# Where two kinds of stores stand in a cross-attention and MLP kernel: block 14's weight sums, and a tile of tokens at the end of a batch

## The chip, the core and the metric

The kernel runs on one core of a Trainium2 chip. The core has TensorE (PE, matrix products into PSUM; its weight loads are a row of their own, PEld), VectorE (DVE), ScalarE (ACT), GpSimd (POOL), and SyncE (SP), which here only issues DMA transfers. Sixteen DMA engines move the data for all of them. Each engine works through its own instructions in order, and waits on semaphores for the others.

The metric is the device time of one execution in microseconds (us), the median of several runs. Everything is computed in float32.

## The reference

A cross-attention block followed by an MLP, with B = 4 batches, L = 512 tokens, D = 512 features, 16 heads of 32 features, and an inner size of 2048:

```python
x = layer_norm(hidden_states, ln1_w, ln1_b)
q = heads(x @ q_w + q_b)
k = heads(encoder_hidden_states @ k_w + k_b)
v = heads(encoder_hidden_states @ v_w + v_b)
attn = softmax(mask(q @ k.T * scale))
hidden = (attn @ v).merge() @ cproj_w + cproj_b + hidden_states
y = layer_norm(hidden, ln2_w, ln2_b)
y = gelu(y @ fc_w + fc_b) @ proj_w + proj_b
return hidden + y
```

## The kernel before

The attention runs in 32 blocks, numbered p = 0 to 31. A block is half of the queries of one head group: w = p // 2 counts batch and group (four groups of four heads in each batch), and p % 2 is the half. `block` (from L349) computes the scores and their softmax (`soften`), and transposes the probabilities on DVE into a tile tb. The blocks leave TensorE time for other matrix work, so each block has a list of fillers (`put(p, ...)`): the projections of the next head groups, `cproj`, and, from block 11 on, the MLP of batch 0 and half of that of batch 1. A filler is a function; what stands in a list is issued in that order, and this sets the order on every engine.

A block's probabilities are used two blocks later. `attend(w, half)` multiplies them with v (tile av, L429). Before, `copies` (from L397) moves tb into a tile pT: four copies within the same partitions on POOL (L405), and twelve DMA transfers across partitions on SP's queue (L410). There is one pT tile for most pairs, so the copies of pair p - 1 start when `attend` of pair p - 2 has read the tile, at the opening of block p. The loop over p at the end of `xattn_block` does this at each opening: `run(ahead[p])`, `attend` of the pair that is due, `fc_sums`, then the block itself.

The MLP's products are made by Winograd's form of Strassen's method: seven half-size products in place of eight, with sums of the operands made beforehand. Four steps matter here.

- `fc_sums` (L704) makes, for a pair of chunks of fc_w (raw in pbt), four sums of weights on POOL: three go to one of the two buffers of wsum, and one replaces a part of the raw chunk. For batch 0 the sums are also stored to DRAM (`sums_dram`, tile ws), with two DMA transfers issued from POOL: L714 with 384 KB, L715 with 128 KB. There are eight pairs, so sixteen such transfers. They are loaded again for batches 2 and 3 (L841), long after. `fc_sums` keeps up to two pairs ahead of the products.
- `fc_by_pair` uses the sums on TensorE (q, L671), and `load_mlp` then loads the next weights into the place of the used ones (L614, on SP's queue).
- `proj_sums` (called by `pre(...)`) makes the sums of the projection's operands on POOL: x and y into ptt, and differences in place into gt and pbt. In block 14 the filler `pre(0, 0)` is last in the list; `x1` just before it issues four loads of the next batch's tokens on SP's queue (L187).
- `proj` for batch 0 issues the seven products q1j to q7j (L777) in block 15 and adds them to the result. At quarter 3 two of the adds are put off by `S["late"]`, and block 29 calls them.

Block 10 calls `fc_sums` as a filler and makes the sums of the first two pairs there; the later pairs are made at the openings of the blocks.

After the attention, `last_mlps` runs the rest of batch 1's MLP and batches 2 and 3. Its second matrix product, `project`, is split once more: for batches 2 and 3 each of the seven products is itself made of seven, by `forty_nine` (from L889; L904 is its matmul). Its results go to three PSUM tiles of four quarters each and to r34: r1 and r26 come from one set of four banks (`acc_tile`), r57 and r34 from the other (`half_tile`, four tiles in turn). The last call in a batch is the one with `parts`: it adds each quarter straight to the result, where `parts` are the four 128 by 128 pieces of 256 tokens and 256 features (two pieces to a tile of 128 tokens). Behind it two transfers (L1028) store these pieces, one for each 128 tokens.

Of the kernel before, what the change touches and what calls it, by code (L numbers as in the profile page):

```python
# [20 lines left out]
P = 128  # L21
# [32 lines left out]
def xattn_block(ctx: ExitStack, tc: tile.TileContext, x, rawT, encT, mask, q_w, k_w, v_w, c_w, fc_w, p_w, vecs, rows, out):  # L54
    nc = tc.nc
# [44 lines left out]
    def mlp_w(n):  # L100
        return pbt[:, (n + MW) * D : (n + MW + 1) * D]
# [16 lines left out]
    S = {"gelu": [], "late": []}  # L118
# [472 lines left out]
    for name, b, i, *_ in products:  # L591
        n = 2 if name == "fc" else FQ
        done += 2 if name == "fc" else 1
        n = range(i * n, (i + 1) * n)
        if (name, b) == ("p", 0) and _[0] == 2:
            n = n[2:]
# [3 lines left out]
    n = next(i for i, w in enumerate(weights) if w[:2] == ("p", SPLIT))  # L600
    weights[n : n + FQ] = weights[n + 2 : n + FQ] + weights[n : n + 2]
    free = [
        next((o[3] for o in reversed(weights[:i]) if o[4] == w[4]), -1) for i, w in enumerate(weights)
    ]

    def load_mlp(most=len(weights)):

        end = min(count[0] + most, len(weights))
        while count[0] < end and free[count[0]] < count[1]:
            name, b, f, _, n = weights[count[0]]  # L610
            w = mlp_w(n)
            if name == "fc":
                w = w.rearrange("p (d f) -> p d f", d=ND)
            Q[0].dma_start(out=w, in_=fc_w[:, f, :, :] if name == "fc" else p_w[ts(f, P), :])  # L614
            S[name + "w", b, f] = w if name == "fc" else n + MW
            count[0] += 1

    NP = NF // 2
    HL = L // 2
# [4 lines left out]
    def add(engine, o, x0, x1):  # L624
        engine.tensor_tensor(o, x0, x1, ALU.add)  # L625

    def a_sums(a11, a12, a21, a22, s1, s2, s3, s4, engine=None):
        add(engine or nc.vector, s1, a21, a22)
        sub(s3, a11, a21, engine)
        sub(s2, s1, a11, engine)  # L630
        sub(s4, a12, s2, engine)
# [66 lines left out]
    sums_dram = dram.tile([NP, P, 4, 2, P], F32, tag="ws", name="ws")  # L698
    fc_pairs = [(0, c) for c in range(NP)] + [(SPLIT, c) for c in range(FIRST * FQ // 2)]

    def raw_pair(b, c):
        return [S["fcw", b, 2 * c + i] for i in range(2)]

    def fc_sums(ahead=2):  # L704

        while count[3] < len(fc_pairs) and count[3] < count[4] + ahead:
            b, c = fc_pairs[count[3]]
            if ("fcw", b, 2 * c + 1) not in S:
                return
            x, y = raw_pair(b, c)  # L710
            s = wsum[:, count[3] % 2]
            a_sums(x[:, :2], x[:, 2:], y[:, :2], y[:, 2:], s[:, 0], s[:, 1], y[:, :2], s[:, 2], nc.gpsimd)
            if b == 0:
                nc.gpsimd.dma_start(out=sums_dram[c, :, :3], in_=s)  # L714
                nc.gpsimd.dma_start(out=sums_dram[c, :, 3], in_=y[:, :2])  # L715
            S["ws", b, c] = s[:, 0], s[:, 1], y[:, :2], s[:, 2]
            count[3] += 1

    def fc_by_pair(b, c):
        q, k = divmod(2 * c, FQ)  # L720
        fc_seven(b, c, gT[q % 2][:, k : k + 2, :], raw_pair(b, c), S["ws", b, c], acc_half, q % 2)
        count[1] += 2
        count[4] += 1
        if (b, c) != (SPLIT, 2):
            load_mlp()
# [105 lines left out]
    def store_out(b):  # L831
        for t in range(NT):
            nc.sync.dma_start(out=out[b, ts(t, P), :], in_=S["hid", b, t])
# [15 lines left out]
    def last_mlps():  # L849
# [8 lines left out]
        p1p, u2p, u3p = (last.tile([P, 2, HL], F32, tag=n, name=n) for n in ("p1p", "u2p", "u3p"))  # L858
# [7 lines left out]
        def more(i):  # L866
            if i == 5:
                return S["more"]
            return [w_more[:, 4 * n : 4 * n + 4] if i == 4 else tt[:, i, n] for n in range(3)]

        def quarters(m):
            return [m[:, i * NP // 2 : (i + 1) * NP // 2, ts(j, P)] for i in range(2) for j in range(2)]
# [13 lines left out]
            sub(x21, x11, x21)  # L886
            sub(s4, x12, s2, nc.gpsimd)

        def forty_nine(b, name, o, x, w, free, i, parts=None):  # L889

            x11, s3, x12, x22 = quarters(x)
            s1, s2, s4 = free if isinstance(free, list) else quarters(free)[:3]
            w11, t3, w21, w22 = quarters(w)
            t1, t2, t4 = more(i)
            r1, r26 = (acc_tile(f"{n}{name}_{b}").rearrange("p (i n) -> p i n", i=4) for n in ("r1", "r26"))
            r57, r34 = (
                half_tile(f"{n}{name}_{b}").rearrange("p i (j n) -> p (i j) n", j=2) for n in ("r57", "r34")
            )
            o = o.rearrange("p t (j n) -> p (t j) n", j=2)
            p1 = p1s[:, i % 2]  # L900

            def product(r, x, w):
                for c in range(NP // 2):
                    nc.tensor.matmul(r, x[:, c], w[:, c], start=(c == 0), stop=(c == NP // 2 - 1))  # L904

            product(r1[:, 0], x11, w11)
            nc.scalar.copy(p1, r1[:, 0])
            product(r26[:, 0], x12, w21)
            product(r26[:, 1], s2, t2)
            add(nc.vector, o[:, 0:4:3], r26[:, :2], p1[:, None, :].broadcast_to([P, 2, P]))  # L910
            product(r57[:, 1], s3, t3)
            product(r57[:, 0], s1, t1)
            add(nc.vector, o[:, 1:3], r57[:, :2], o[:, 3:4].broadcast_to([P, 2, P]))
            add(nc.vector, o[:, 3], r57[:, 0], o[:, 2])
            if parts:
                for n, h in enumerate(parts):
                    add(nc.vector, h, o[:, n], h)
            product(r34[:, 0], s4, w22)
            product(r34[:, 1], x22, t4)
            if parts:  # L920
                for n in (1, 2):
                    add(nc.vector, parts[n], r34[:, n - 1], parts[n])
                return
            add(nc.vector, o[:, 1:3], r34[:, :2], o[:, 1:3])

        def half_tile(name):
# [11 lines left out]
        def project(b, pairs, sums, turns, middle):  # L938
            g11, g12, g21, g22 = (ga[:, :, k, j * HL : (j + 1) * HL] for j in range(2) for k in range(2))
            b11, b12, b21, b22 = (pb[:, :, k, j * HL : (j + 1) * HL] for k in range(2) for j in range(2))  # L940
            t1, t2, t3, t4 = pt[:, 0], pt[:, 1], b12, pt[:, 2]
            s1, s2, s3, s4 = gs[:, 0], gs[:, 1], g21, gs[:, 2]
# [8 lines left out]
            def hid(i, j, t):  # L951
                return S["hid", b, 2 * i + t][:, j * HL : (j + 1) * HL]
# [70 lines left out]
            if b > SPLIT:  # L1023
                parts = [hid(1, 0, t)[:, ts(j, P)] for t in range(2) for j in range(2)]
                middle()
                forty_nine(b, "4", u2p, g22, t4, s3, 5, parts)
                for t in range(2):
                    nc.sync.dma_start(out=out[b, ts(2 + t, P), :HL], in_=hid(1, 0, t))  # L1028
                return
            middle()  # L1030
            q4 = half_tile(f"q4p_{b}"), acc_half(f"q4p_{b}")
# [15 lines left out]
        for b, pairs, new in (  # L1047
            (SPLIT, range(half, NP), range(half)), (SPLIT + 1, range(NP), ()), (SPLIT + 2, range(NP), ())
        ):
            for c in pairs:  # L1050
# [6 lines left out]
                if new:  # L1057
                    n = (c - half + 2) % half
# [44 lines left out]
    def do(fn):  # L1103
        return [(0.0, fn)]
# [81 lines left out]
    def some(n):  # L1186
        taken = []
        while n > 0:
            n -= 1 if mlp[0][0] == CHAIN else 2
            taken.append(mlp.pop(0))  # L1190
        assert n == 0
        return taken

    def pre(b, q, sides="aw"):
        return do(lambda: proj_sums(b, q, sides))
# [24 lines left out]
    def put(p, *work, before=(), mid=()):  # L1220

        work = [item for part in work for item in part]
        ahead[p], mids[p] = list(before), list(mid)
        fills[p] = work
# [13 lines left out]
    x1, x2, x3, x4 = inputs(2)  # L1238
    k, q, v = A(7)
    c, t2 = C(0), turns2(0)  # L1240
# [4 lines left out]
    k, q, v = A(8)  # L1245
    put(10, [k], norm(0, 0, 1), [v], norm(0, 2, 3), do(fc_sums), [q], t2)
    k, q, v = A(9)
    put(11, [k, v], some(2), pb_(0), mid=do(lambda: y_sums(0)))

    x1, x2, x3, x4 = inputs(3)  # L1250
    put(12, [q], some(2))
    k, q, v = A(10)
    put(13, [k], some(2))
    put(14, [q], some(2), x1, pre(0, 0))
    put(15, some(1), x2[:1], V(10, True), x2[1:2], do(lambda: load_raw(3)), some(2), do(lambda: (store_rn(3), load_rn(3))))

    k, q, v = A(11)
    put(16, do(lambda: ln1_rows(3, *range(ND))), [k, q], some(2), h_(1, 0, 1))
    put(17, next_(lambda: ln1_affine(3)), h_(1, 2, 3), x4, cb(1), C(1))
    k, q, v = A(12)  # L1260
    put(18, [q], some(2), pre(0, 1))
    k12 = k
    k, q, v = A(13)
# [3 lines left out]
    k, q, v = A(14)  # L1267
    t2 = turns2(1)
    put(22, [k, q], norm(1, 0, 1), some(2), norm(1, 2, 3), pre(0, 2))
    k15, q15, _ = A(15)  # L1270
    put(23, some(1), [k15], t2, pb_(1), h_(2, 2, 3, 0, 1))
    c = C(2)
# [2 lines left out]
    put(26, c[3:], do(lambda: attend(12, 0)), pre(0, 3, "w"), some(1))  # L1275
    put(27, some(3))
    put(28, some(3))
    put(29, some(1), do(lambda: (fc_sums(), S["late"].pop()())), some(2), do(lambda: (store_out(0), load_mlp())))
    between[14, 1] = lambda: load_mlp(2)
    put(30, some(3), mid=hid_(1, 2, 3))  # L1280
    put(31, some(3))
# [3 lines left out]
    for p in range(2 * NW):  # L1285
        w, half = divmod(p, 2)
        if half == 0 and w and w % NG == 0:
            make_mb(w // NG)
        run(ahead[p])
        for pair in due.get(p, ()):  # L1290
            attend(*divmod(pair, 2))
        if p > 10:
            fc_sums(1 if p == 29 else 2)
        while held_back:
            held_back.pop(0)()

        def fill(n, work=fills[p]):
            if n or not work or work[0][0] <= CHAIN:
                run(work, CHAIN if n < 2 else None)

        block(w, half, fill, any(cost > CHAIN for cost, _ in fills[p]), mids[p])
# [6 lines left out]
    c = cproj_last()  # L1308
# [59 lines left out]
```

## Time and profile before

| | us |
|---|---|
| median of 3 runs | 755.61 |
| the runs | 755.61, 758.24, 755.61 |
| the profiled execution | 758.21 |
| its span, first to last instruction | 756.4 |
| outside its span | 1.8 |

The times of single instructions come from the profiled execution alone. A row of a timeline gives the start within the span, the length, the engine, the line of the kernel, the operation, the output and the inputs, the shapes and a count; equal instructions that follow each other share a row. In brackets stands the time that the engine was idle before the row, with what ended it by the profile: where an instruction waits for several things, the one that came last by the profile's account is named, which need not be the one that mattered. "SPq" is the sync queue: its rows are the issue of transfers, not their data. The rows in the section on DMA give the data by queue: q1 is the hardware queue, filled from SP and ACT, and q0 the software queue, filled from POOL.

### The profile page before, as it was taken

What the parts mean: (1) busy time and instruction counts of PE and PEld (TensorE: products, weight loads), DVE (VectorE), ACT (ScalarE), POOL (GpSimd) and SP (SyncE); (2) the same over time, 40 slices, a digit from 0 to 9 for tenths busy, and PEclk for the clock granted to TensorE, in tenths of its full rate; (3) what the DMA queues carried; (4) which work ended last, traced back from release to release, by engine and by line L of the source; (5) the groups of instructions that cost most, each with busy time, mean ns of one, the idle gap of its engine ahead of it and who ended that gap; (6) DMA issues with size and microseconds to landing.
All of it is one profiled execution on the core that took longest, in us unless ns stands there. A gap on an engine that the chain in (4) does not pass through costs nothing.

```text
span 756.4 us, 13322 instructions
## 1 busy us (share of the span) xinstructions
PE 748.7 (99%) x4514; PEld 536.2 (71%) x4514; DVE 617.6 (82%) x1229; ACT 341.0 (45%) x776; POOL 403.6 (53%) x401
## 2 busy tenths in 40 slices
PE   9999999999999999999999999999999999999997
PEld 6655555567567546675655776468888899988997
DVE  3889999879988779877987999949877987956865
ACT  2566766555874475648853578401302211022200
POOL 1536837468687987667868974532150014403153
PEclk9999999999999999999999999999999999999999
DMA  8988989467796797676756757766634402046001
GB/s 326 348 238 223 248 208 257 107 191 185 210 255 208 199 268 182 169 193 156 196 129 198 195 145 242 187 213 234 242 104 152 155 13 91 29 162 201 1 15 43
DMA packets 60836, 134.62 MB, mean 178 GB/s; under 512 B 11312, under 2 KB 17072, under 8 KB 60640
## 3 DMA queue, kind: packets, MB, share of 16 engines
q1 hardware_dynamic: 59024, 127.78, 58.7%
q0 software_dynamic: 1600, 5.97, 2.6%
q8 instruction: 36, 0.59, 0.3%
q14 instruction: 32, 0.26, 0.1%
q10 hardware_dynamic: 144, 0.02, 0.0%
HBM read 69.23 MB, written 11.02 MB: 106 GB/s over the span
## 4 chain that ended last, share of the span: by engine, by line
PE 95%; POOL 3%; DMA 1%; issue 0%; SPq 0%; DVE 0%; DVEq 0%; POOLq 0%
PE q L671 24%; PE r L904 10%; PE sc L329 8%; PE av L429 7%; PE acck L262 7%; PE accq L274 7%; PE accc L471 6%; PE accv L285 5%; PE accp L758 4%; PE accv L310 3%; PE q1p L965 2%; PE tp L169 1%; POOL pT L405 1%; PE q3j L777 1%; PE q1j L777 1%; PE q7j L777 1%
## 5 line engine op out<-in xcount | busy, mean ns | idle before, releaser
L339 ACT ACTIVATE ptt<-ptt,mn 128x512 f32<-128x512 f32 x256 | 181.7, 711 | 142.3 <-DVE mn L335 142.3
L335 DVE CUSTOM_DVE_ANT_0 ptt<-sc,mb 128x512 f32<-128x512 f32 x256 | 160.6, 682 | 19.9 <-PE sc L329 19.9
L347 DVE STREAM_TRANSPOSE tb<-ptt 128x1024 f32<-128x1024 f32 x128 | 153.3, 1217 | 0.0
L405 POOL COPY pT<-tb 32x1088 f32<-32x1088 f32 x96 | 104.7, 1091 | 35.1 <-DVE oT L434 11.6
L671 PE MATMUL q<-yT,gt 128*128 128x256 f32 x320 | 78.9, 379 | 0.0
L692 ACT ACTIVATE ga<-ga,vec 128x512 f32<-128x512 f32 x40 | 26.7, 714 | 93.3 <-DVE ga L625 93.3
L671 PEld LDWEIGHTS q<-yT,gt 128*128 128x128 f32 x320 | 60.7, 190 | 8.2
L329 PE MATMUL sc<-pbt 32*128 32x512 f32 x512 | 66.1, 614 | 0.0
L671 PE MATMUL q<-ys,gt 128*128 128x256 f32 x240 | 61.6, 379 | 0.0
L262 PE MATMUL acck<-xe,ptt 128*128 128x512 f32 x128 | 59.1, 605 | 0.0
L274 PE MATMUL accq<-xe,ptt 128*128 128x512 f32 (+1 forms) x136 | 58.1, 573 | 0.0
L671 PEld LDWEIGHTS q<-ys,gt 128*128 128x128 f32 x240 | 45.6, 190 | 6.2
L625 DVE TENSOR_TENSOR ga<-q,ga 128x512 f32<-128x512 f32 (+1 forms) x60 | 36.2, 603 | 15.8 <-PE q L671 12.9
L429 PE MATMUL av<-pT,v 128*32 128x256 f32 x768 | 46.4, 382 | 2.1 <-POOL gt L622 1.9
L339 ACT ACTIVATION_READ_ACCUMULATOR ptt<-ptt,mn 128x1 f32 x256 | 47.8, 187 | 0.0
L274 PEld LDWEIGHTS accq<-xe,ptt 128*128 128x128 f32 x136 | 25.0, 190 | 30.4 <-issue 23.0
L440 POOL TENSOR_TENSOR hid<-hid,row 128x512 f32<-128x512 f32 x18 | 23.5, 1332 | 42.2 <-DMA hid<-xa 42.2
L262 PEld LDWEIGHTS acck<-xe,ptt 128*128 128x128 f32 x128 | 23.4, 192 | 31.6 <-issue 23.0
L329 PEld LDWEIGHTS sc<-pbt 32*128 32x128 f32 x512 | 27.2, 183 | 25.5 <-issue 17.2
L471 PE MATMUL accc<-wc,oT 128*128 128x512 f32 x96 | 42.5, 597 | 0.0
L285 PEld LDWEIGHTS accv<-ptt,xe 128*128 128x128 f32 x320 | 37.0, 192 | 4.9 <-DVE mn L335 2.7
L321 POOL TENSOR_TENSOR v<-v,row 128x512 f32<-128x512 f32 x16 | 20.3, 1280 | 37.1 <-ACT v L290 29.7
(263 smaller groups left out, 1437.2 us busy)
## 6 DMA issues: line engine op xcount, KB each, us to landing
pT<-tb SPq DMA_DIRECT2D x288, 136.0 KB
pbt<-p_w_dram SPq DMA_DIRECT2D x40, 256.0 KB
gt<-ws SPq DMA_DIRECT2D x20, 512.0 KB
gt<-tb SPq DMA_DIRECT2D x48, 136.0 KB
xe<-tb SPq DMA_DIRECT2D x48, 136.0 KB
pbt<-fc_w_dram SPq DMA_DIRECT2D x24, 256.0 KB
gt<-fc_w_dram SPq DMA_DIRECT2D x20, 256.0 KB
ptt<-k_w_dram SPq DMA_DIRECT2D x16, 256.0 KB
```

The costliest lines, as they stand in the source:

```text
L262: nc.tensor.matmul(acc, S["wk", w][:, d, :], eT[:, d, :], start=(d == 0), stop=(d == ND - 1))
L274: nc.tensor.matmul(acc, S["wq", w][:, d, :], xT[:, d, c], start=(d == 0), stop=(d == ND - 1))
L285: nc.tensor.matmul(acc[:, ts(t, P)], eT[:, d, ts(t, P)], S["wv", w][:, d, :], start=(d == 0), stop=(d == ND - 1),)
L329: nc.tensor.matmul(S["sc", w, qt][h], qT[r, ts(qt, P)], kT[r, :], start=True, stop=True)
L335: nc.vector.tensor_tensor_reduce(out=s, in0=S["sc", w, qt][h], in1=S["mb", w // NG], scale=1.0, scalar=FMAX, op0=ALU.add, op1=ALU.min, acc ...
L339: nc.scalar.activation(s, s, AF.Exp, bias=mn, scale=-1.0, accum_out=S["sums", w][:, qt, h : h + 1])
L347: nc.vector.transpose(tv[:, qt % 2, 2 * k : 2 * k + 2], S["ps", w, qt, k])
L405: nc.gpsimd.tensor_copy(pT[ts(i, HD), i], tb[ts(i, HD), i])
L429: nc.tensor.matmul(av[ts(h, HD), : 2 * P].rearrange(shape, **kw), v[:, t, ts(h, HD)], p[t][h], start=(t == 0), stop=(t == NT - 1),)
L471: nc.tensor.matmul(acc, S["oT", b][:, g, ts(t, P)], wc[:, g, :], start=(g == 0), stop=(g == NG - 1))
L671: nc.tensor.matmul(o, x[:, k], y[:, k], start=(k == 0), stop=(k == 1))
L904: nc.tensor.matmul(r, x[:, c], w[:, c], start=(c == 0), stop=(c == NP // 2 - 1))
```

## The change

The stores of weight sums become entries of `S["late"]`, and a function `late` issues what is in that list. The loop over p calls it right behind `fc_sums`, in every block from 11 on but block 14; there it stands at the end of the fillers, behind `pre(0, 0)`.

On POOL two places change. In blocks 10 and 11, the sums of the first two pairs follow each other, and their four stores stand behind the four copies into pT. In block 14, the two stores of the fifth pair move behind the four sums of the projection's operands. The put-off adds of quarter 3 keep their place.

In `forty_nine` with `parts`, the seventh small product gets a tile r4 of its own in place of a quarter of r34. On DVE the order of the last six adds becomes: pieces 0 and 1, piece 1 again with r34, pieces 2 and 3, piece 2 again with r4. The first tile of 128 tokens is stored behind the third of them, the second behind the last. TensorE's products keep their order.

```diff
             if b == 0:
-                nc.gpsimd.dma_start(out=sums_dram[c, :, :3], in_=s)
-                nc.gpsimd.dma_start(out=sums_dram[c, :, 3], in_=y[:, :2])
+                S["late"].append(lambda c=c, s=s, y=y: (
+                    nc.gpsimd.dma_start(out=sums_dram[c, :, :3], in_=s),
+                    nc.gpsimd.dma_start(out=sums_dram[c, :, 3], in_=y[:, :2]),
+                ))
             S["ws", b, c] = s[:, 0], s[:, 1], y[:, :2], s[:, 2]
             count[3] += 1
+
+    def late():
+        while S["late"]:
+            S["late"].pop(0)()
...
-        def forty_nine(b, name, o, x, w, free, i, parts=None):
+        def forty_nine(b, name, o, x, w, free, i, parts=None, ready=None):
...
             if parts:
-                for n, h in enumerate(parts):
-                    add(nc.vector, h, o[:, n], h)
+                r4 = half_tile(f"r4{name}_{b}").rearrange("p i (j n) -> p (i j) n", j=2)
+                for n in (0, 1):
+                    add(nc.vector, parts[n], o[:, n], parts[n])
+                product(r34[:, 0], s4, w22)
+                add(nc.vector, parts[1], r34[:, 0], parts[1])
+                ready(0)
+                for n in (2, 3):
+                    add(nc.vector, parts[n], o[:, n], parts[n])
+                product(r4[:, 0], x22, t4)
+                add(nc.vector, parts[2], r4[:, 0], parts[2])
+                ready(1)
+                return
             product(r34[:, 0], s4, w22)
             product(r34[:, 1], x22, t4)
-            if parts:
-                for n in (1, 2):
-                    add(nc.vector, parts[n], r34[:, n - 1], parts[n])
-                return
             add(nc.vector, o[:, 1:3], r34[:, :2], o[:, 1:3])
...
-                forty_nine(b, "4", u2p, g22, t4, s3, 5, parts)
-                for t in range(2):
-                    nc.sync.dma_start(out=out[b, ts(2 + t, P), :HL], in_=hid(1, 0, t))
+                forty_nine(
+                    b, "4", u2p, g22, t4, s3, 5, parts,
+                    lambda t: nc.sync.dma_start(out=out[b, ts(2 + t, P), :HL], in_=hid(1, 0, t)),
+                )
                 return
...
-    put(14, [q], some(2), x1, pre(0, 0))
+    put(14, [q], some(2), x1, pre(0, 0), do(late))
...
-    put(29, some(1), do(lambda: (fc_sums(), S["late"].pop()())), some(2), do(lambda: (store_out(0), load_mlp())))
+    put(29, some(1), do(lambda: (fc_sums(), late())), some(2), do(lambda: (store_out(0), load_mlp())))
...
         if p > 10:
             fc_sums(1 if p == 29 else 2)
+            if p != 14:
+                late()
```

## The prediction

> **What bounds the kernel now.** I read the page first (shares of busy time and the chain that ended last), then the table of TensorE's waits, then the engines' timelines around each wait and at the end.
>
> ```profile
> span 756.4 us, 13322 instructions
> ...
> PE 748.7 (99%) x4514; PEld 536.2 (71%) x4514; DVE 617.6 (82%) x1229; ACT 341.0 (45%) x776; POOL 403.6 (53%) x401
> ...
> PE 95%; POOL 3%; DMA 1%; issue 0%; SPq 0%; DVE 0%; DVEq 0%; POOLq 0%
> ```
>
> TensorE is busy for 748.7 of 756.4 us and carries 95% of the chain. The change issues the same matmuls in the same order, so all that can move is TensorE's idle time and what follows its last matmul. The table of its waits has three rows in all:
>
> ```profile
> PE av L429 <- POOL gt L622: 1.9, 1, 1.9
> PE warm L1157 <- POOL ident masks.py:199: 1.3, 1, 1.3
> PE av L429 <- POOL raw L221: 0.2, 1, 0.2
> ```
>
> One wait is large, and the timeline puts it at the opening of block 15 (rows of PE, the sync queue and POOL, start and length in us):
>
> ```profile
> 206.15 8.47 SPq L410 DMA_DIRECT2D pT<-tb  x12
> 214.08 0.56 POOL L714 DMA_DIRECT2D ws<-wsum  x1 [0.30 <-POOL wsum L622]
> 214.65 0.54 POOL L715 DMA_DIRECT2D ws<-pbt  x1
> 215.20 1.29 POOL L625 TENSOR_TENSOR ptt<-gt 128x512 f32<-128x512 f32 x1
> ...
> 218.89 1.27 POOL L622 TENSOR_TENSOR pbt<-pbt 128x512 f32<-128x512 f32 x1
> 216.16 1.03 PE L671 MATMUL q<-ys,pbt 128*128 128x256 f32 x4
> 219.04 1.93 PE L429 MATMUL av<-pT,v 128*32 128x256 f32 x32 [1.86 <-POOL gt L622]
> ```
>
> The profile names POOL's subtraction into gt, but this product reads neither that nor anything made from it. Among what it reads is pT of pair 13, whose twelve copies across partitions left the sync queue from 206.15 to 214.62. TensorE was free at 216.16 + 1.03 = 217.19 and started 1.86 us later, 219.04 - 214.62 = 4.42 us after the last copy was issued. The other wait of that kind is in block 17, where no store of POOL's stands beside the copies:
>
> ```profile
> 247.44 9.58 SPq L410 DMA_DIRECT2D pT<-tb  x12
> 259.20 1.93 PE L429 MATMUL av<-pT,v 128*32 128x256 f32 x32 [0.21 <-POOL raw L221]
> ```
>
> There the product starts 259.20 - 257.02 = 2.18 us after the last issue. So the last copy of pair 13 is some 2.2 us late. The DMA view from 215.0 to 217.5 says beside what:
>
> ```profile
> DMA packets 115, 0.49 MB, mean 196 GB/s; under 512 B 22, under 2 KB 22, under 8 KB 115
> q1 hardware_dynamic: 66, 0.20, 51.2%
> q0 software_dynamic: 49, 0.29, 41.2%
> ```
>
> The software queue is POOL's: block 14's store of sums, issued at 214.08, takes 0.29 of 0.49 MB just while the last copies drain. That is the stall.
>
> **The change, part by part.**
>
> *Block 14's stores behind the sums of the projection's operands.* Two issues leave the place at 214.08; they hold 215.20 - 214.08 = 1.12 us. The four sums follow directly and end at 220.16 - 1.12 = 219.04, and the stores are issued from there to 220.16. No packet of theirs stands before 219. How much of the stall goes? Lower bound: the 0.29 MB at 196 GB/s is 1.5 us of DMA time; taken off 219.04 that leaves a start at 217.5, 0.3 us after TensorE is free, so 1.5 us gained. Upper bound: by block 17's 2.18 us the copy is there at 214.62 + 2.18 = 216.8, before 217.19, and all 1.86 us go. I take 1.86: the second row is the same product behind the same twelve copies. The Trainium skill, page "DMA: Bandwidth & Descriptors", section on the anatomy of one DMA, fits a transfer (one issued from POOL) at about 2.0 us plus its bytes over 436 GB/s; for one copy's 136 KB that is an estimate of 2.3 us, by which the copy lands by 216.9 and the gain is again the whole 1.86 us, with the cover down to 0.3 us.
>
> What the stores now stand before on POOL, and what they collide with:
>
> ```profile
> 221.58 4.48 POOL L405 COPY pT<-tb 32x1088 f32<-32x1088 f32 x4 [1.41 <-DVE oT L434]
> 221.54 7.87 SPq L410 DMA_DIRECT2D pT<-tb  x12
> 242.02 1.93 PE L429 MATMUL av<-pT,v 128*32 128x256 f32 x32
> ```
>
> With TensorE 1.86 us earlier, POOL's copies of pair 14 could start at 219.72; POOL is free at 220.16, so they lag by 0.44 us. Their reader is at 242.02 - 1.86 = 240.16, while the sync queue had issued the last one by 229.41. Even if the 0.29 MB and the rest of the 512 KB of stores all delay these copies (512 KB at 196 GB/s, 2.7 us), some 8 us are left. I cost it at nothing; without that cover it would be up to 2.7 us.
>
> *Blocks 10 and 11.* Here the sums of two pairs are made without a store between, and all four stores stand behind the copies of pT:
>
> ```profile
> 162.08 0.64 POOL L714 DMA_DIRECT2D ws<-wsum  x1 [0.30 <-POOL wsum L622]
> 163.29 0.74 POOL L625 TENSOR_TENSOR wsum<-pbt 128x256 f32<-128x256 f32 x1
> 166.96 0.56 POOL L714 DMA_DIRECT2D ws<-wsum  x1 [0.30 <-POOL wsum L622]
> 168.06 4.69 POOL L405 COPY pT<-tb 32x1088 f32<-32x1088 f32 x4
> 175.56 1.27 POOL L321 TENSOR_TENSOR v<-v,row 128x512 f32<-128x512 f32 x1 [2.81 <-ACT v L290]
> 173.12 4.02 SPq L614 DMA_DIRECT2D pbt<-p_w_dram  x2
> 179.22 7.51 SPq L410 DMA_DIRECT2D pT<-tb  x12
> 190.18 1.93 PE L429 MATMUL av<-pT,v 128*32 128x256 f32 x32
> DMA to landing us min/median/max: 2.8/4.5/5.4
> ```
>
> POOL's work adds up to the same: the copies start 1.21 + 1.10 = 2.31 us sooner, at 165.75, end at 170.44, and four issues bring POOL to 172.75, where it stood before its 2.81 us of idle time. Nothing on POOL is late. One reader is: the second load of a projection weight at 173.12 overwrites the first pair's raw chunk, and so waits for the second store as well as for TensorE; its issue ended at 177.14. That store is now issued at about 171.1 and, by the landing row, has landed by 175.6 (at most 176.5). Cover 0.6 us to the end of the issue that TensorE releases; after it the sync queue has no work until 179.22. Cost: nothing. All other stores keep their order.
>
> *Two banks for the last two products.* At the end of batch 3:
>
> ```profile
> 751.07 0.88 DVE L625 TENSOR_TENSOR hid<-u2p,hid 128x128 f32<-128x128 f32 x4
> 751.09 1.06 PE L904 MATMUL r<-row,ga 128*128 128x128 f32 x8
> 752.19 0.49 DVE L625 TENSOR_TENSOR hid<-r,hid 128x128 f32<-128x128 f32 x2 [0.23 <-PE r L904]
> 752.54 0.81 SPq L1028 DMA_DIRECT2D out_dram<-hid  x2
> L1028 SPq DMA_DIRECT2D out_dram<-hid x2: 333/353/373, 752.5 to 753.0; - x2
> ```
>
> Both adds from PSUM wait for the last matmul (752.15), though the first needs only the product that ended before 751.3; both stores follow. With a bank of its own the first add moves into the row of four, and its store goes out near 751.9. Behind the last matmul stands one add, 752.19 to 752.48, and one issue at 752.54 in place of the one at 753.0: 0.44 us. Five dependent adds instead of four fill DVE until about 752.3, so the lower bound is 0.3 us; I take 0.42.
>
> The same edit runs at the end of batch 2, where TensorE goes on:
>
> ```profile
> 661.82 0.48 DVE L625 TENSOR_TENSOR hl<-r,hl 128x128 f32<-128x128 f32 x2
> 664.39 1.03 PE L671 MATMUL q<-ys,gt 128*128 128x256 f32 x4
> ```
>
> One more tile shifts the rotation of four banks by one. The first product that then takes a bank of this sum starts near 664.4, over 2 us after DVE's last read of it. Nothing.
>
> *Block 17.* The next wait on the path is the 0.21 us at 259.20. What feeds it:
>
> ```profile
> 240.20 1.89 PE L777 MATMUL q4j<-pbt,gt 128*128 128x256 f32 x8
> 242.74 0.20 DVE L206 STREAM_TRANSPOSE rnT<-rn 128x32 f32<-128x32 f32 x1
> 246.52 0.82 SPq L216 DMA_DIRECT2D hid<-rn  x2
> ```
>
> The transpose stands on DVE behind the add of q4j, which ends with TensorE at 242.1; its store, the reload at 246.52 and the twelve copies at 247.44 follow in turn. All of it moves with TensorE, and the 0.21 us stays.
>
> Sum: 1.86 + 0.42 = 2.28 us (bounds 1.5 + 0.3 = 1.8 and 1.86 + 0.44 + 0.21 = 2.5). The profiled execution, 758.21 us with 756.4 inside the span, would give 755.9 with a span of 754.1. Two of the three timed runs took 755.61 us, 2.6 less than the profiled one and the third. Taken off the median the sum gives 755.61 - 2.28 = **753.3 us**.
>
> **The rivals.**
>
> *The shorter runs have no stall.* The gap of 2.6 us between runs is near 1.86 + 0.21 plus a little. If it is this race of copy and store that some executions win, the median already lacks the stall and only the tail is gained: 755.61 - 0.42 = 755.2. Against it: POOL's place for the stores is the same in every execution, and they last for over 2 us.
>
> *The gain is given back in block 17.* If the store and reload of rn or the copies at 247.44 do not follow TensorE, av stays at 259.20: again 755.2. For it: the chain of waits goes through them. Against it: they start from TensorE's own q4j.
>
> *Slower: the sync queue blocked in block 11.* If four stores in a row land late, the second load at 173.12 holds the queue, and with it the twelve copies at 179.22. These end at 186.73, plus 2.18 is 188.9, against a reader at 190.18: it decides from a landing after 180.5, and each us beyond costs one. It outweighs the sum from 182.8 on, 11.7 us after the issue, against 5.4 at most so far. With a landing at 185 the time is 755.61 + 4.5 - 2.28 = 757.8.
>
> *The edit does nothing for pT.* If the last copy waits for something else (the weight loads behind it on the sync queue), the stall stays: 755.2 too; the 0.29 MB speak against it.
>
> **How the numbers follow.** Forecast 0.63; no stall in the shorter runs 0.16; given back 0.06; the edit without effect on pT 0.06; slower 0.04; the remaining 0.05 for medians that fall on different groups of runs (758.2 before against 753.3 after would be 0.65%). Half a per cent, about what a measurement can tell from no change, is 3.8 us, more than all of TensorE's idle time after its start. The likeliest case has 752.8 to 754.0 for itself. The range goes from 752.6 to 756.0: it takes in the 755.2 of three rivals and an after in the longer group (758.2 - 2.28). Faster by over 0.5%: 0.10, from the mixed medians and a little for what I don't see; slower: 0.03; within: 0.87.
>
> **What would show it.** Right: no wait of av behind q at block 15 (219.04 becomes 217.2), POOL's stores at 219.0, TensorE's waits down to the start and some 0.2 us, block 17's av near 257.3, one add behind the last matmul and the second store's issue 0.44 us sooner against it. Wrong: av still over 0.5 us late in block 15 or a larger wait at block 17; a wait of the sync queue for a store in block 11; a TensorE wait that before does not have.

## The result and the profile after

| | before | after |
|---|---|---|
| median of 22 runs each | 756.37 | 757.88 |
| lowest and highest | 755.57, 761.25 | 757.26, 760.26 |
| the profiled execution | 758.21 | 757.92 |
| its span | 756.4 | 756.1 |

The ratio of the times is 1.0019, with a 95% interval of 1.0010 to 1.0028. The kernel became 1.5 us slower, where 2.3 us less was predicted. The two profiled executions say the opposite (756.1 against 756.4), since that of before has the wait of block 15 in it and most of its runs do not: this is part of the answer below.

The page of the changed kernel, busy time by engine, the chain that ended last, and two of its groups:

```profile
span 756.1 us, 13324 instructions
...
PE 750.9 (99%) x4514; PEld 537.5 (71%) x4514; DVE 619.8 (82%) x1229; ACT 341.0 (45%) x776; POOL 403.1 (53%) x401
...
PE 99%; DVE 0%; issue 0%; POOL 0%; POOLq 0%; DVEq 0%
...
L329 PE MATMUL sc<-pbt 32*128 32x512 f32 x512 | 68.7, 616 | 0.0
```

The table of TensorE's waits has one row left (line waited at, releaser; us in total, times, longest):

```profile
PE warm L1170 <- POOL ident masks.py:199: 1.3, 1, 1.3
```

Both waits of av are gone, and yet TensorE is "busy" for 750.9 us where it was 748.7, with the same 4514 matmuls at a granted clock of 1.00. Its 99% of the chain is no proof of useful work either. The group of the scores (tile sc) holds the difference. Before it read:

```profile
L329 PE MATMUL sc<-pbt 32*128 32x512 f32 x512 | 66.1, 614 | 0.0
```

512 matmuls took 2.6 us more, while the mean of one went from 614 to 616 ns, which accounts for 1.0 us at most. So most of it is not longer matmuls, but matmuls that no longer run side by side. The timeline gives the place, block 12 (first the changed kernel, then the kernel before; start, length, engine):

```profile
177.08 1.93 PE L429 MATMUL av<-pT,v 128*32 128x256 f32 x32
178.94 3.80 PE L329 MATMUL sc<-pbt 32*128 32x512 f32 x16
```

```profile
178.57 2.00 PE L329 MATMUL sc<-pbt 32*128 32x512 f32 x16
```

The same sixteen matmuls take 3.80 us in place of 2.00. That is 1.80 us in one spot, where no wait is listed for PE. In the kernel before they start in fours, each four within 0.02 us. In the changed kernel the last eight start one at a time (from 179.90 to 182.15), so that one or another is running all the time, and the profile counts the stretch as busy. The engine named by PE's weight loads there is DVE (waits of PEld, 177 to 183 us, of the changed kernel):

```profile
PEld sc L329 <- DVE gt L625: 0.7, 2, 0.4
```

So DVE's adds into gt are late. Followed backwards on DVE and POOL, the changed kernel (rows of two timelines):

```profile
165.07 5.58 POOL L405 COPY pT<-tb 32x1088 f32<-32x1088 f32 x4
165.51 1.19 DVE L622 TENSOR_TENSOR ys<-yT 128x512 f32<-128x512 f32 x1
166.81 1.39 DVE L622 TENSOR_TENSOR ys<-yT,ys 128x512 f32<-128x512 f32 x1
168.12 1.57 DVE L622 TENSOR_TENSOR yT<-yT 128x512 f32<-128x512 f32 x1
169.62 1.57 DVE L622 TENSOR_TENSOR ys<-yT,ys 128x512 f32<-128x512 f32 x1
171.12 0.68 DVE L335 CUSTOM_DVE_ANT_0 ptt<-sc,mb 128x512 f32<-128x512 f32 x1
...
179.29 1.95 DVE L625 TENSOR_TENSOR gt<-q,gt 128x512 f32<-128x512 f32 x3
```

and the kernel before:

```profile
165.14 0.93 DVE L622 TENSOR_TENSOR ys<-yT 128x512 f32<-128x512 f32 x1
166.18 1.03 DVE L622 TENSOR_TENSOR ys<-yT,ys 128x512 f32<-128x512 f32 x1
167.13 0.68 DVE L622 TENSOR_TENSOR yT<-yT 128x512 f32<-128x512 f32 x1
167.73 0.68 DVE L622 TENSOR_TENSOR ys<-yT,ys 128x512 f32<-128x512 f32 x1
168.34 0.68 DVE L335 CUSTOM_DVE_ANT_0 ptt<-sc,mb 128x512 f32<-128x512 f32 x1
...
176.51 1.95 DVE L625 TENSOR_TENSOR gt<-q,gt 128x512 f32<-128x512 f32 x3
```

These four sums of y are made by DVE from two inputs in SBUF each. Before, the stores of the first two pairs kept POOL's copies into pT away until 168.06, when the last of these sums had begun. With the stores behind the copies, the copies run from 165.07 to 170.65, beside all four sums. Each side slows the other: the sums take 171.12 - 165.51 = 5.61 us from the first start to the next operation, where it was 168.34 - 165.14 = 3.20, and the copies 5.58 where it was 4.69. DVE is 2.4 us late from there on, through the softmax work that follows, to the adds into gt (179.29 against 176.51, of which 0.37 us is a later start of the whole execution). TensorE loses 1.80 of them, so some 0.6 us were in hand. DVE's operations that read PSUM or one input from SBUF are not touched. The one at 168.34 of the kernel before stands beside the copies and takes the same 0.68 us as the one at 171.12 of the changed kernel, where they have ended.

The Trainium skill has this rule on the page "SBUF — State Buffer", section "Who interferes with whom": a DVE instruction with two SBUF inputs contends with a GpSimd instruction that reads SBUF, and one with at most one SBUF input, outside the modes of DVE that use both of its ports, does not. The trace agrees on which operations are hit. For those modes the page has one side blocked for the whole instruction of the other. The trace shows something near it for these sums: the two sides take turns. In the changed kernel each sum ends 0.54 to 0.55 us after the end of the copy beside which it started, and a copy that starts while a sum is running takes 1.46 us in place of 1.09. So both sides grew, a sum by up to 0.89 us (0.68 to 1.57).

Where each execution gained or lost time can be read from the starts of the same product av at the opening of a block. This table is worked out from rows of the timelines: start of av less its start in the third of the further runs of the kernel before (b3 below, an execution with no wait of av at all), in us, at the openings of blocks.

| | block 12 | 13 | 15 | 16 | 17 | near 304 us |
|---|---|---|---|---|---|---|
| start in b3 | 176.89 | 190.35 | 217.29 | 240.27 | 257.17 | 304.46 |
| before, the first profile | -0.18 | -0.17 | 1.75 | 1.75 | 2.03 | 2.02 |
| after | 0.19 | 1.99 | 1.99 | 1.99 | 2.00 | 2.14 |

The kernel before lost 1.9 us at block 15 in its first profile; the kernel after loses 1.80 at block 12. Neither does both. Of four profiles of the kernel before, two have the loss at block 15; the loss at block 12 is in both profiles of kernels with the first pairs' stores behind the copies.

The tail, changed kernel (rows of PE, DVE and the sync queue):

```profile
751.22 1.06 PE L910 MATMUL r<-row,ga 128*128 128x128 f32 x8
751.78 0.29 DVE L625 TENSOR_TENSOR hid<-r,hid 128x128 f32<-128x128 f32 x1
751.99 0.48 DVE L625 TENSOR_TENSOR hid<-u2p,hid 128x128 f32<-128x128 f32 x2
752.39 0.28 DVE L625 TENSOR_TENSOR hid<-r,hid 128x128 f32<-128x128 f32 x1
752.14 0.94 SPq L1040 DMA_DIRECT2D out_dram<-hid  x2
```

One add starts behind the last matmul (752.28), and the issue of the second store ends 752.14 + 0.94 - 752.28 = 0.80 us after it, where it was 752.54 + 0.81 - 752.15 = 1.20. From the last matmul to the end of the span it is 3.86 us, before 4.27.

### The profile page after: what moved, and what is told of

Read it like the earlier page. It is cut to its first block, busy times and chain, and to the rows that moved or that the text cites. A ratio compares the mean times of both kernels' runs of the same rounds, so it can differ in the third digit from the quotient of the medians.

```text
span 756.1 us, 13324 instructions
## 1 busy us (share of the span) xinstructions
PE 750.9 (99%) x4514; PEld 537.5 (71%) x4514; DVE 619.8 (82%) x1229; ACT 341.0 (45%) x776; POOL 403.1 (53%) x401
## 4 chain that ended last, share of the span: by engine, by line
PE 99%; DVE 0%; issue 0%; POOL 0%; POOLq 0%; DVEq 0%
PE q L671 26%; PE r L910 10%; PE sc L329 9%; PE av L429 8%; PE acck L262 8%; PE accq L274 7%; PE accc L471 6%; PE accv L285 5%; PE accp L764 4%; PE accv L310 3%; PE q1p L977 2%; PE tp L169 1%; PE q1j L783 1%; PE q3j L783 1%; PE q6j L783 1%; PE q2j L783 1%
## 5 line engine op out<-in xcount | busy, mean ns | idle before, releaser
L329 PE MATMUL sc<-pbt 32*128 32x512 f32 x512 | 68.7, 616 | 0.0
```

What stands on the lines that cost most here:

```text
L329: nc.tensor.matmul(S["sc", w, qt][h], qT[r, ts(qt, P)], kT[r, :], start=True, stop=True)
```

## The experiments

**The first two pairs stored at once.** The whole change, but for the stores of blocks 10 and 11, which stay where they were.

```diff
                     nc.gpsimd.dma_start(out=sums_dram[c, :, 3], in_=y[:, :2]),
                 ))
+                if count[3] < 2:
+                    late()
```

> The changed kernel, but with the first two pairs' stores issued as before, each right behind its sums; block 14 and the two banks stay changed. Theory (POOL's copies of pT run beside DVE's four sums of y in block 11 and hold them up): the four sums take 0.7 to 1.0 us each again, the scores of block 12 lose their 2.2 us, nothing waits at block 15, and the end is 0.4 us sooner: about 755.3 us, 0.6 to 1.0 below before's 756.4. Rival (the loss comes from block 14's move or from the fifth tile): still some 757.9 us.

Measured: 756.35 us against 757.91 for the kernel before, ratio 0.9977 (0.9964 to 0.9990). The loss at block 12 is gone, and the sums are as before, the third and fourth at 0.68 us too (DVE's timeline, the first two):

```profile
165.22 0.93 DVE L622 TENSOR_TENSOR ys<-yT 128x512 f32<-128x512 f32 x1
166.25 1.03 DVE L622 TENSOR_TENSOR ys<-yT,ys 128x512 f32<-128x512 f32 x1
```

So what makes the changed kernel slower is the moved stores of these two pairs, and the rest of the change is a gain. This version beats both kernels.

**The four stores together, but ahead of the copies.** The stores of both pairs are put off as in the change, yet issued at the opening of block 11, before POOL's copies.

```diff
+        if p == 11:
+            late()
         run(ahead[p])
```

> The changed kernel, but the four stores of the first two pairs are issued in a row behind both pairs' sums and ahead of POOL's copies into pT, instead of behind them. Theory (copies beside DVE's sums): the four issues now stand beside the sums of y, which take about 0.7 us each, the first two less than before's 0.93 and 1.03; block 12 loses nothing; about 755.3 us. Rival (four stores in a row crowd the DMA engines and block the sync queue, which waits for one of them before a weight load): as slow as the changed kernel, about 757.9 us.

Measured: 756.69, ratio 0.9979 (0.9965 to 0.9993). This takes apart the two things that the change did to DVE's sums. Its timeline:

```profile
165.69 0.64 POOL L715 DMA_DIRECT2D ws<-wsum  x1
...
167.94 4.97 POOL L405 COPY pT<-tb 32x1088 f32<-32x1088 f32 x4
166.12 0.69 DVE L622 TENSOR_TENSOR ys<-yT 128x512 f32<-128x512 f32 x1
...
167.52 0.69 DVE L622 TENSOR_TENSOR yT<-yT 128x512 f32<-128x512 f32 x1
168.12 1.58 DVE L622 TENSOR_TENSOR ys<-yT,ys 128x512 f32<-128x512 f32 x1
...
179.55 2.00 PE L329 MATMUL sc<-pbt 32*128 32x512 f32 x16
```

The three sums beside the issues take 0.69 us each; the fourth, of the same shape and beside the copies, 1.58. One kernel holds both prices. The whole stretch is 169.62 - 166.12 = 3.50 us, 0.3 more than before, which lies within the 0.6 us in hand: the scores of block 12 have their 2.00 us. The time is lost by what runs beside the sums, not by the order of the stores among themselves.

**Only the first two pairs' stores moved.** The kernel before with this part alone.

```diff
-                nc.gpsimd.dma_start(out=sums_dram[c, :, :3], in_=s)
-                nc.gpsimd.dma_start(out=sums_dram[c, :, 3], in_=y[:, :2])
+                store = lambda c=c, s=s, y=y: (
...
+                S["late"].append(store) if count[3] < 2 else store()
...
             fc_sums(1 if p == 29 else 2)
+            if p == 11:
+                while S["late"]:
+                    S["late"].pop(0)()
```

> The kernel before with one part of the change: the first two pairs' stores behind the copies into pT in block 11. Theory: DVE's sums of y at 1.2 to 1.6 us each and TensorE's scores in block 12 2.2 us late, so 756.4 + 2.2 = 758.6 us, less what the later wait of block 15 gives back where it occurs. Rival (the loss is elsewhere): 756.4 us, no difference.

Measured: 758.89, ratio 1.0019 (1.0007 to 1.0032). The loss is made by this part alone (groups of DVE from 164 to 172 us: busy, mean ns):

```profile
L622 DVE TENSOR_TENSOR ys<-yT,ys 128x512 f32<-128x512 f32 x2 | 3.0, 1483 | 0.1
L622 DVE TENSOR_TENSOR yT<-yT 128x512 f32<-128x512 f32 x1 | 1.6, 1575 | 0.0
L622 DVE TENSOR_TENSOR ys<-yT 128x512 f32<-128x512 f32 x1 | 1.2, 1196 | 0.0
```

Against b3, av is 0.14 us late at the opening of block 12 and 1.95 at that of block 13. The profiled execution took 762.42 us, the longest of its twelve, since it also has the wait of block 15, and something behind it (timeline of PE):

```profile
221.51 3.31 PE L429 MATMUL av<-pT,v 128*32 128x256 f32 x32 [2.20 <-DVE gt L625]
224.75 2.26 PE L329 MATMUL sc<-pbt 32*128 32x512 f32 x16
```

After the wait of 2.20 us, av takes 3.31 us in place of 1.93 and the scores 2.26 in place of 2.00, 1.64 us more. Up to 221.5 the granted clock is 1.00. The windows after it give the reason (columns: stretch and length, busy time of PE, PEld, DVE, ACT and POOL, granted clock, DMA share, GB/s):

```profile
221.50:223.00 1.50, 1.49 (x20) 1.05 (x24) 0.00 (x0) 0.56 (x1) 0.78 (x1) 0.64 1.03 365
223.00:224.80 1.80, 1.80 (x24) 0.68 (x15) 0.00 (x0) 0.00 (x0) 0.00 (x0) 0.50 1.05 393
224.80:227.00 2.20, 2.20 (x19) 0.92 (x17) 1.25 (x4) 0.09 (x1) 1.55 (x2) 0.88 0.62 198
```

**Only block 14's stores moved.** The kernel before with this part alone.

```diff
+                S["late"].append(store) if count[3] == 4 else store()
...
-    put(14, [q], some(2), x1, pre(0, 0))
+    put(14, [q], some(2), x1, pre(0, 0), do(lambda: S["late"].pop(0)()))
```

> The kernel before with one part of the change: block 14's two stores behind the sums of the projection's operands. If the wait at block 15 occurs in only some executions of before (its runs at 757.3 to 758.3 us, six of 22), the times lose that upper group and the median falls by 0.2 to 0.6 us, to about 756.0; if it is in every execution, by 1.9 us, to 754.5. Rival (this part costs time): above 756.4 us.

Measured: 757.09 against 757.91, ratio 0.9985 (0.9970 to 0.9999). No wait of av in its profile, where av starts as q ends and the store follows:

```profile
216.44 1.93 PE L429 MATMUL av<-pT,v 128*32 128x256 f32 x32
218.00 0.56 POOL L715 DMA_DIRECT2D ws<-wsum  x1
```

**Only the two banks.** The kernel before with the edit of `forty_nine` alone, as in the diff of the change.

```diff
-        def forty_nine(b, name, o, x, w, free, i, parts=None):
+        def forty_nine(b, name, o, x, w, free, i, parts=None, ready=None):
...
+                r4 = half_tile(f"r4{name}_{b}").rearrange("p i (j n) -> p (i j) n", j=2)
```

> The kernel before with one part of the change: the last two small products in two banks, each half stored as it is ready. Theory: behind the last matmul one add in place of two and the second store's issue 0.4 us sooner; nothing else moves; 0.3 to 0.45 us less, a ratio of 0.9995 (below what such runs tell apart, so the profile's end decides). Rival (the fifth tile makes TensorE wait at the start of batch 3, or the split stores cost at the end): no gain, or some tenths lost, and a wait of TensorE near 660 us in the profile.

Measured: 756.41 against 756.81, ratio 1.0005 (0.9990 to 1.0019): the times can't tell 0.4 us from nothing. The profile can, since it has the stretch by itself: 3.86 us from the last matmul to the end of the span, in this kernel and in the changed one, against 4.27 to 4.29 in four profiles of the kernel before. Nothing new waits at the end of batch 2. The stretch alone is not proof: the two profiles of the doubled store below have 3.85 us without this edit, since POOL's closing instructions come sooner in them. But the issue of the second store ends 1.20 us after the last matmul in all eight profiles without the edit, and 0.79 or 0.80 in all five with it.

**The kernel before, three times more.** No edit; each time another execution is profiled.

> The kernel before, unchanged, profiled again. Theory (the wait at block 15 is a race that goes differently from one execution to the next): its length differs from the 1.86 us of the first profile, between 0 and 2 us. Rival (it is in every execution): 1.8 to 1.9 us again.

> The kernel before, unchanged, a third profile. As for the second: a wait at block 15 anywhere from 0 to 2 us by the theory of a race, 1.8 to 1.9 us by the rival.

> The kernel before, unchanged, a fourth profile. As for the second: a wait at block 15 anywhere from 0 to 2 us by the theory of a race, 1.8 to 1.9 us by the rival.

Measured, b1 to b3: 755.97, 758.66 and 756.21 us. The first has one wait of av, 0.5 us near 304 us. The second has (TensorE's waits):

```profile
PE av L429 <- POOL gt L622: 2.0, 1, 2.0
...
PE av L429 <- DMA ptt<-k_w_dram: 0.5, 1, 0.5
```

and the third none. The wait of 0.5 us is the one near 304 us again. In block 15 it is 1.86 in the first profile of before, then 0, 1.99 and 0. In the third, POOL issues the store at the old place, and av follows its q without a gap:

```profile
214.25 0.56 POOL L714 DMA_DIRECT2D ws<-wsum  x1 [0.30 <-POOL wsum L622]
217.29 1.93 PE L429 MATMUL av<-pT,v 128*32 128x256 f32 x32
```

So the wait comes in some executions and not in others, and the ones with it are the longer ones.

**Block 14's first store twice.** If the store's data make the copies late, more of it must make the wait certain. The kernel before, with 384 KB more issued right behind; two executions, the first kernel also timed.

```diff
                 nc.gpsimd.dma_start(out=sums_dram[c, :, :3], in_=s)
+                if count[3] == 4:
+                    nc.gpsimd.dma_start(out=sums_dram[c + 1, :, :3], in_=s)
```

> The kernel before with one store more: in block 14 the fifth pair's 384 KB of sums are sent a second time, right behind the first store (to the place of the sixth pair, which that pair's own store overwrites later). Six profiles without the move of block 14's stores had the wait of av at block 15 three times (1.86, 1.99 and 2.20 us), four with the move not once; by chance alone that is not rare. Theory (the store's data delays the last copies into pT): with 0.9 MB in place of 0.5 MB beside the copies every profile shows the wait, at 2 us or more, by up to 384 KB / 196 GB/s = 2.0 us longer than before's, and the median is 1 to 4 us above before's. In the profile of the first-pairs-late kernel a wait of 2.20 us was followed by a granted clock of 0.64 and 0.50 for some 3.4 us, which cost 1.6 us more; after 1.86 and 1.99 us it stayed at 1.00. If the length of the wait decides, that shows here too. Rival (the wait comes from the sync queue's own pace, and the store beside it is no cause): a wait in about half the profiles, of 1.9 to 2.2 us at most, and a ratio of 1.000 (POOL's 0.6 us for the issue is covered by the scores before q1j, or costs up to 0.3 us).

> The same kernel once more, for a second profile. Theory: the wait of av at block 15 again, over 2 us. Rival: present or absent as chance has it, 2.2 us at most.

Measured: 756.94 against 757.41, ratio 0.9994 (0.9983 to 1.0005), and 755.96 for the second. Neither has a wait in block 15 (the first has one of 0.71 us at block 17). The rows of the first (in the second, av starts at 217.31 with the second store at 214.83):

```profile
206.63 7.80 SPq L410 DMA_DIRECT2D pT<-tb  x12
214.55 0.56 POOL L714 DMA_DIRECT2D ws<-wsum  x1 [0.30 <-POOL wsum L622]
215.11 0.54 POOL L716 DMA_DIRECT2D ws<-wsum  x1
...
217.59 1.93 PE L429 MATMUL av<-pT,v 128*32 128x256 f32 x32
```

The expectation of the theory failed. It does not speak against the store's data, though, since in neither execution did these come ahead of the copy. The last copy's issue ended at 206.63 + 7.80 = 214.43, 0.12 us before even the first store was issued; in the second profile it was 0.04 us. More data behind the last copy could not test whether data ahead of it make it late.

**The same second store, at the late place**, in the kernel that stores the first two pairs at once.

```diff
                     nc.gpsimd.dma_start(out=sums_dram[c, :, :3], in_=s),
+                    c == 4 and nc.gpsimd.dma_start(out=sums_dram[c + 1, :, :3], in_=s),
```

> The same second store in the kernel that has the whole change but stores the first two pairs at once: both 384 KB stores stand behind the four sums of the projection's operands. Theory: no wait of av at block 15, and the time of that kernel (0.998 of before's, 0.996 to 1.000), plus up to 0.6 us for the issue ahead of POOL's copies. Rival: the wait is there in about half of the profiles whatever the place of the stores.

Measured: 756.26, ratio 0.9983 (0.9972 to 0.9993), without a wait in block 15 (av waits 1.01 us near 304 us). As a control it says little, since the early place showed none either.

**What tips the wait of block 15.** Of eight profiles with block 14's stores at the old place three have it (1.86, 1.99, 2.20 us), of five with the stores moved none. If the place had no influence, all three would fall among the eight in one case of five (8·7·6 / (13·12·11) = 0.20), so the count alone doesn't show that the move removes it. What does tell the three apart is the sync queue's issue of the twelve copies. In the first profile of before (8.47 us, in the prediction), in the second further run and in the kernel with the first pairs late it took over 8.3 us; the longest without the wait took 8.15. From the second further run, with the store, and from the third, whose store is shown above:

```profile
206.16 8.39 SPq L410 DMA_DIRECT2D pT<-tb  x12
214.09 0.56 POOL L714 DMA_DIRECT2D ws<-wsum  x1 [0.30 <-POOL wsum L622]
```

```profile
206.33 8.01 SPq L410 DMA_DIRECT2D pT<-tb  x12
```

This is a race between two engines. The queue's first copy and POOL's own copies start together at the opening of the block, and POOL's way from there to the store is steady: in all eight profiles with the old place the store is issued 7.92 to 7.94 us after the queue's first issue. The queue needs 7.80 to 8.50 us for its twelve. The trace also holds the start of every DMA packet and the time of every semaphore update, and these show who comes first on the DMA engines (us after the end of the last copy's issue, least to most):

| | old place, wait (3 profiles) | old place, no wait (5) | stores moved (5) |
|---|---|---|---|
| the first store is issued | -0.57 to -0.47 | -0.21 to 0.12 | 4.36 to 4.76 |
| its first data packet starts | 0.81 to 0.92 | 1.29 to 2.48 | 6.23 to 7.40 |
| the copy's last packet starts | 2.42 to 2.76 | 1.17 to 1.20 | 1.18 to 1.20 |
| the copy has landed | 4.01 to 4.33 | 1.89 to 2.32 | 1.77 to 1.78 |

Where the store's first data come ahead of the copy's last packets, these start over a us late and the copy lands more than 2 us late; av follows 0.41 us after the landing in each of the three. The eleventh copy, with no store's data near it, has landed 1.75 to 1.82 us after its issue in all thirteen. So the wait does come from the store's data, as the prediction read it, and with the stores moved these come 5 us and more too late to disturb the copy. An execution with the stores moved and the queue as slow as in the three is not among the profiles.

What makes the queue slow in some executions stays open. Taken one by one, most of its issues stand 0.63 us apart. Between the second and the third it is 1.40 to 1.45 us in the three executions with the wait and 0.64 to 1.29 in the ten without (the one with 0.64 has 1.28 at the next place); and between the ninth and the tenth it is 0.74 to 0.87 in the three, 0.63 or 0.64 in the ten. The first place is at 207 to 209 us, some seven us ahead of block 14's stores, so it is not these that slow the queue.

The times say a little more. The four kernels with block 14's stores moved and no loss in block 12 have 0.9977, 0.9979, 0.9983 and 0.9985, all with intervals below 1 (the first three also have the two banks, 0.41 of 756 us or 0.0005); the two with the stores at the old place and no loss in block 12 have 1.0005 and 0.9994, both with 1 inside. Block 14's part is thus worth some 0.1 to 0.2%, which is what a wait of 1.9 us or more in some half of the runs would come to. How many runs have it may differ between groups of runs: the kernel before has medians of 756.37, 757.91, 756.81 and 757.41 us in the four groups.

## Why the prediction was wrong, step by step

- *Block 14's stores, 1.86 us off the median.* The mechanism was right: where av waits, the store's data stand ahead of the last copy's packets, and the copy lands 4.01 us after its issue in place of 1.78, the "some 2.2 us late" of the prediction. The step that failed is that the term was taken off the median: executions of about the length of that median (755.97 and 756.21 us among the further runs) have no such wait. The rival "the shorter runs have no stall" was right on this, in its own words a race of copy and store. Its objection, that POOL's place for the stores is the same in every execution, was wrong: the place in the program is, but the store is issued some 0.5 us ahead of the end of the last copy's issue in b2 and 0.1 in b3, and the wait is 1.99 and 0.
- *Blocks 10 and 11, "Nothing on POOL is late. Cost: nothing."* **This step decided the sign:** what was put at nothing cost 1.80 us. That its end times for POOL were near is luck (the copies end at 170.65, predicted 170.44; the fourth issue at 172.85, predicted 172.75): the copies started at 165.07 in place of 165.75 and took 5.58 us in place of 4.69. The step asked only who is late on POOL, and which transfer is late, not what else runs where the copies now stand. The four sums of y on DVE stood there, and the copies starting 3 us sooner cost DVE 2.4 us and TensorE 1.80. A sign of it was in the trace of before: POOL's sum at 165.60 took 1.06 us and DVE's beside it 0.93 and 1.03, where each takes 0.73 and 0.69 alone.
- *The second load of the projection weight.* It did wait for the second store (wait of the sync queue, then the issue of the loads; changed kernel):

```profile
SPq L614 <- DMA ws<-pbt: 2.2, 1, 2.2
172.90 4.61 SPq L614 DMA_DIRECT2D pbt<-p_w_dram  x2
```

  That store was issued at 171.25 and landed at 175.41, by the trace's semaphore updates, near the 171.1 and 175.6 of the prediction. TensorE released the load after that: its issue ended at 177.51, where it was 177.14 in an execution that stood 0.37 us earlier, and the queue issued nothing more until 181.59. The cost of nothing was right. The slower rival's example of 757.8 us, for a store that lands at 185, is near the measured median by chance: the loss did not come that way.
- *Two banks, 0.42 us.* Measured 0.41 in the profiles. The stores and the one add came as described, and batch 2 has no new wait.
- *Block 17, 0.21 us.* It follows no edit: it is absent in the changed kernel, 0.44 us in the kernel with the first pairs at once and 0.71 in the first profile of the doubled store. It varies between executions, as the wait of block 15 does; what makes it vary was not followed.
- *The sum.* For an execution without waits of av it is 1.80 - 0.41 = 1.39 us more. The lowest runs differ by 757.26 - 755.57 = 1.69, the medians by 1.51. The forecast of 753.3 had 1.86 of gain that an execution of the median's length could not give, and lacked 1.80 of loss. The range ended at 756.0, since none of the rivals held a loss of an engine by another's neighbourhood. Nor did its list of signs hold it: most signs of being right came, with no wait of av at block 15 and TensorE's waits down to the start, and the one sign of being wrong that came, the sync queue's wait for a store, cost nothing.

## What to carry to other kernels

When instructions move on one engine, lay what comes forward over the other engines' timelines and look for pairs that already slow each other: two sums that take 1.0 us here and 0.7 there are such a sign. A wait that stands in one profile is one draw; before its length is taken off a median, look whether the median run has it. Where two engines race, ask which came first in each execution before an experiment is read: the doubled store came behind the copy, and so could not test the theory. And a loss can hide in "busy": compare the length of equal runs of matmuls, not only the table of waits.

## What the runs showed of the hardware

- **DVE and POOL on SBUF.** A DVE sum of 128x512 with two SBUF inputs takes 0.68 us alone or beside the issue of transfers, 0.93 to 1.03 beside POOL's sums, and up to 1.58 beside POOL's copies of 32x1088. POOL's four copies take 4.5 us alone, 4.69 to 5.58 beside such sums. The two take turns: a sum ends 0.54 to 0.55 us after the copy beside which it started.
- **A store from POOL beside a copy from the sync queue.** The last packets of a 136-KB copy start by 1.20 us after its issue, and it has landed 1.77 to 1.78 us after it with no store near. Where the 384-KB store's first data come earlier than that, at 0.81 to 0.92 us, the copy's last packets start at 2.42 to 2.76, and it lands at 4.01 to 4.33.
- **The clock after a short wait.** In one execution TensorE stood for 2.20 us, and the granted clock then averaged 0.64, 0.50 and 0.88 in three stretches: at one half that is (0.36·1.5 + 0.50·1.8 + 0.12·2.2) / 0.5 = 3.4 us, which cost 1.64 us. After 1.86 us in the first profile of before, the clock did not move (windows, same columns):

```profile
219.00:220.00 1.00, 0.96 (x20) 0.75 (x24) 0.21 (x1) 0.94 (x1) 1.00 (x1) 1.00 0.95 342
```

  Nor did it after 1.99 us. The Trainium skill, page "TensorE: Matmul & The Clock Gate", section "Part 1: The HAM clock gate", has half the clock after an idle window of about 3.4 us, and windows of that length. The length of the slow stretch agrees; here it came after a shorter wait. In these executions such a wait thus cost 1.9 or 3.8 us, and this may be in the longest runs of the kernel before (up to 761.25), though none of those was profiled.
- **The start.** Executions of one kernel stand up to 0.8 us apart at the same matmul by 177 us (0.82 between two runs of the kernel before), with no wait in the table of waits. It is half of what the change as a whole came to.
